# Two steps' attention sums in one run, and a state space's narrow products padded to 128

## The chip, the cores and the metric

The kernel runs on one core of a Trainium2 chip. The metric is the device time of one execution in microseconds. A core has a matrix engine (PE, with its weight loads listed apart as PEld), a vector engine (DVE), a scalar engine for activation functions (ACT), a general engine (POOL), a queue engine (SP), and DMA queues. The engines run side by side and wait for one another through semaphores. Products are written to PSUM, which has eight banks here; everything else lies in SBUF.

## The reference

Two layers over one sequence of 2048 positions with 128 channels, all in 32-bit floating point. Each of four blocks normalises, computes and adds to the residual:

```python
x = x + L0_attn(layernorm(x))   # state space, 8 heads of 32, state 16, gated
x = x + L0_ffn(layernorm(x))    # causal attention, 16 heads of 8, then 8 experts
x = x + L1_attn(layernorm(x))   # second state space, 256 channels, state 16
x = x + L1_ffn(layernorm(x))    # feed-forward, 512 hidden
```

The change touches the first state space and the attention. Their cores are:

```python
# state space, per position t
h = exp(dt*A) * h + dt * x_t[..., None] * B_t          # B_t, C_t: 16 values
y_t = einsum('bhpn,bn->bhp', h, C_t) + D * x_t
# attention
scores = einsum('bqhd,bkhd->bhqk', q, k) / sqrt(8)     # causal mask
out = einsum('bhqk,bkhd->bqhd', softmax(scores), v)
```

## The kernel before

The sequence is cut into four chunks c of 512 positions, each of four blocks of 128. A tile framework turns the program, written in the order of its priorities, into one list of instructions for each engine, with waits; within an engine the list runs in order.

**Stages.** First the state space (`ssd(c)`) for chunks 0 and 1 runs alone, with the preparation of attention for chunk 0. Then the state space for chunks 2 and 3 runs beside the attention of chunks 0 and 1; `abreast` deals out turns to both in proportion to their lengths. Then the attention of chunks 2 and 3 runs alone, with small extra pieces (the preparation of chunk 3, output products, the experts' gates). Experts, second state space and feed-forward follow.

**State space.** Within a chunk, the scan is done block by block with matrix products. For each block b: four products of 128 rows (taps of the convolution, L623) and one product of a single row, which adds the bias `cb_half` (L624), make `xbc`, 288 wide: 256 channels, 16 columns of B, 16 of C. B and C are transposed by products with 16 weight columns (L645) into `bcT`, 16 partitions high. Their product (L649) contracts over 16 rows; 128-row products make the decay matrix (L640) and the output within the block (L665). The product with the old state (L671) contracts over 16 rows; the new state (L678) is a product with 16 weight columns. In a trace the shape of a product is given as rows*columns of the array that it uses: 1*128, 16*128, 128*16 and 128*128. `xbc` and `bcT` come from the pool of work tiles, `state` from the pool of small tiles, each with two buffers.

**Attention.** Heads go in groups g of four (NG = 4 groups). `prepare(c)` writes keys `kR` and queries `qR`, laid out so that each head has 32 rows. Two threads of work follow.

- `shift` computes the scores of queries against keys once (L311, with a mask product L320 where the chunk is on the diagonal) only for their maxima. VectorE reduces each bank (L317, L321), and `spread` turns the maxima into a row `sh`. The bank is tag `m`: two buffers in the mixed stage, three in attention alone.
- `weighted` goes through the key blocks kb of 128. One step computes transposed scores for four heads, in two pairs (L395), adds the maxima (L401) and on the diagonal a mask (L404), and takes the exponential on ACT (L406) into `probs`. The bank is tag `e`, two buffers, one per pair.

`sum_up` multiplies one step's exponentials by the values, with 9 weight columns per head, or 32 for the first block (L363), and accumulates over the key blocks in the bank of tag `o`. One step has four such products, each of which the hardware's list holds as two instructions. After the last key block the sums are copied out (L369), and `end_group` transposes and divides them (L375, L380).

What sets the order: `attentions` takes one turn of the maxima for each of the six turns of a step, so a step's list on PE is two score products, a maximum's product, two additions of the maxima, another maximum's product, the same for the second pair, and then the sums of the step before, which `weighted` keeps in the list `waiting`:

```python
                if i and waiting:
                    sum_up(*waiting.pop())
            waiting.append((c, g, kb, q0, prs, last))
```

So each step of 160 (16 for each group of chunk 3, 12, 8 and 4 for those of chunks 2, 1 and 0) has one run of sums. `probs` has five buffers: two steps of two, and one more. `qR` has 12 buffers, three chunks of four groups.

Of the kernel before, what the change touches and what calls it, by code (L numbers as in the profile page):

```python
# [12 lines left out]
F32 = mybir.dt.float32  # L13
BF16 = mybir.dt.bfloat16
F32R = mybir.dt.float32r
AF = mybir.ActivationFunctionType
# [56 lines left out]
def two_layers(ctx: ExitStack, tc: tile.TileContext, a: dict, out: bass.AP):  # L73
# [186 lines left out]
    def prepare(c, bank):  # L260

        xn = xa[c] = xp.tile([P, NB, D], F32, tag="xa", name="xa", bufs=4)
        layernorm(xn, xc[c])
        nx = aw.tile([P, NB, D], F32, tag="os", name="nx")
        layernorm(nx, xn)
        nc.gpsimd.tensor_tensor(xn, xn, row("bo").unsqueeze(1).to_broadcast([P, NB, D]), ALU.add)
        pt = transposed(nx, bank)
        nT = aw.tile([P, C], F32, tag="nTa", name="nTa", bufs=1)
        nc.vector.tensor_scalar(nT, pt, col("ln1_w"), col("ln1_b"), ALU.mult, ALU.add)
        yield 1.0  # L270
        pv = bank([P, NB, NH, HD])
        for b in range(NB):
            nc.tensor.matmul(
                pv[:, b].rearrange("p h d -> p (h d)"), nT[:, b * P : (b + 1) * P], w_v, start=True, stop=True
            )
        for b in range(NB):
            kb = c * NB + b
            nc.vector.tensor_tensor(
                (v0 if kb == 0 else vv[:, kb - 1])[:, :, 0:HD], pv[:, b], row("bv").rearrange("p (h d) -> p h d", h=NH), ALU.add
            )  # L280
        yield 1.0
        cs = slice(c * C, (c + 1) * C)
        held[c] = []
        for g in range(NG):
            held[c].append(ap.tile([P, C], F32R, tag="qR", name="qR", bufs=3 * NG))
            for w, n, dst in ((w_k, "k", kR[:, g, cs]), (w_q, "q", held[c][g])):
                pf = bank([P, C])
                nc.tensor.matmul(pf, w[:, g], nT, start=True, stop=True)
                hi = aw.tile([P, C], F32R, tag="os", name="hi")
                nc.scalar.activation(hi, pf, AF.Identity, bias=col(f"b{n}", g))  # L290
                yield 1.0
                nc.tensor.matmul(pf, minus[n], hi, start=False, stop=True, skip_group_check=True)
                nc.vector.tensor_scalar(dst, pf, col(f"b{n}", g), None, ALU.add)
# [89 lines left out]
    def weighted(c, g):  # L383

        qR = held[c][g]
        sh = held.pop((c, g))
        for kb in range((c + 1) * NB):
            diag = kb >= c * NB
            q0 = (kb - c * NB) * P if diag else 0
            prs = []  # L390
            for i in range(0, 4, 2):
                pss = psum("e", [P, 2, C])
                for j in range(2):
                    hr = slice(32 * (i + j), 32 * (i + j) + 32)
                    nc.tensor.matmul(  # L395
                        pss[:, j, q0:], kR[hr, g, kb * P : (kb + 1) * P], qR[hr, q0:], start=True, stop=False
                    )
                yield
                for j in range(2):
                    hr = slice(32 * (i + j), 32 * (i + j) + 32)  # L400
                    nc.tensor.matmul(pss[:, j, q0:], onesR[hr], sh[hr, q0:], start=False, stop=not diag)  # L401
                yield
                for j in range(2 * diag):
                    nc.tensor.matmul(pss[:, j, q0 : q0 + P], ident16, mask_kq, start=False, stop=True)  # L404
                pr = ak.tile([P, 2, C], F32, tag="probs", name="probs", bufs=5)
                last = nc.scalar.activation(  # L406
                    pr[:, :, q0:], pss[:, :, q0:], AF.Exp, scale=float(1.0 / np.sqrt(np.float32(HD)))
                )
                in_turn("exp", last)
                prs.append(pr)  # L410
                yield
                if ending:
                    end_group(*ending.pop())
                if i and waiting:
                    sum_up(*waiting.pop())
            waiting.append((c, g, kb, q0, prs, last))

    def conclude(c):
# [25 lines left out]
    def attentions(*which):  # L444


        if not at["maxima"]:
            take(sizes[0] + LEAD)
        for c, g in which:
            if g == 0 and c:  # L450
                extras.append(conclude(c - 1))
            if (c, g) == (NC - 2, 0):
                extras.append(prepare(NC - 1, lambda shape: psum("m", shape)))
            if (c, g) == jobs[-1]:
                extras.extend(gating(i, lambda shape: psum("m", shape)) for i in range(NC - 1))
            for n, _ in enumerate(weighted(c, g)):
                next(ahead, None)
                if n % 3 < 2:
                    continue
                at["softmax"] += 1  # L460
                at["maxima"] += 1
                if n % 6 == 5:
                    while at["maxima"] + 2 <= np.interp(at["softmax"] + LEAD, starts[:-1], starts[1:]):
                        take(2)
                    if n > 6 and extras and next(extras[0], None) is None:
                        extras.pop(0)
                yield 1.0
        for e in extras:
            for _ in e:
                pass  # L470
        extras.clear()
        sum_up(*waiting.pop())
        end_group(*ending.pop())

    ahead = maxima(jobs)
# [58 lines left out]
    with ExitStack() as first:  # L534
# [9 lines left out]
        w_xbc = load(wp, "w_xbc", [P, XBC])  # L544
        nc.vector.tensor_scalar(w_xbc, w_xbc, 0.5, None, ALU.mult)
        nc.vector.tensor_tensor(w_tap, w_tap, w_xbc.unsqueeze(1).to_broadcast([P, 4, XBC]), ALU.mult)
        cb_half = wp.tile([1, XBC], F32, name="cb_half")
        nc.vector.tensor_scalar(cb_half, row("conv_b", 1), 0.5, None, ALU.mult)
        w_dt = load(wp, "w_dt", [P, NH0])
        w_zx = load(wp, "w_zx", [P, 2 * DI])  # L550
        nc.vector.tensor_scalar(w_zx[:, 0:DI], w_zx[:, 0:DI], 0.5, None, ALU.mult)
# [13 lines left out]
        nc.gpsimd.memset(halo0, 0.0)  # L565

        state = [None]

        big, small_bank = (lambda shape: psum("a", shape)), (lambda shape: psum("c", shape))

# [5 lines left out]
        def ssd(c):  # L576
# [43 lines left out]
            for b in range(NB):  # L620
                pc = big([P, XBC])
                for k in range(4):
                    nc.tensor.matmul(pc, nT[:, b * P + k : (b + 1) * P + k], w_tap[:, k, :], start=k == 0, stop=False)  # L623
                nc.tensor.matmul(pc, ones[0:1, :], cb_half, start=False, stop=True)  # L624
                xbc = work([P, XBC], "xbc", "xbc")
                nc.scalar.activation(xbc, pc, AF.Tanh)
                nc.vector.scalar_tensor_tensor(xbc, xbc, 1.0, pc, ALU.add, ALU.mult)
                xh = xbc[:, 0:DI].rearrange("p (h q) -> p h q", h=NH0)

                r = work([P, NH0, P], "r", "ssd_r")  # L630
# [9 lines left out]
                    nc.tensor.matmul(pr, after, r[:, 4 * j : 4 * j + 4, :].rearrange("p h t -> p (h t)"), start=True, stop=True)  # L640
                    nc.scalar.activation(m[:, 4 * j : 4 * j + 4, :].rearrange("p h t -> p (h t)"), pr, AF.Exp)
                yield 3.6
                pb = small_bank([DS, 2, P])
                for j in range(2):
                    nc.tensor.matmul(pb[:, j, :], xbc[:, DI + j * DS : DI + (j + 1) * DS], ident, start=True, stop=True)  # L645
                bcT = work([DS, 2, P], "bcT", "bcT")
                nc.vector.tensor_copy(bcT, pb)
                pcb = small_bank([P, P])
                nc.tensor.matmul(pcb, bcT[:, 0, :], bcT[:, 1, :], start=True, stop=True)  # L649
                cb = work([P, P], "cb", "cb")  # L650
# [18 lines left out]
                if old is not None:  # L669
# [4 lines left out]
                    yi = work(hd, "yi", "yi")  # L674
                    nc.vector.tensor_tensor(yi, pi, dec[:, 0, b, :].unsqueeze(2).to_broadcast(hd), ALU.mult)
                    nc.gpsimd.tensor_tensor(yb, yb, yi, ALU.add)
                pn = small_bank([DS, NH0, HD0])
                nc.tensor.matmul(  # L678
                    pn.rearrange("p h q -> p (h q)"), xbc[:, DI : DI + DS], xw.rearrange("p h q -> p (h q)"), start=True, stop=True
                )  # L680
                new = sp.tile([DS, NH0, HD0], F32, tag="state", name="state")
                if old is None:
                    nc.vector.tensor_copy(new, pn)
                else:
                    nc.vector.tensor_tensor(
                        new, old, dec[:DS, 1, b, :].unsqueeze(2).to_broadcast([DS, NH0, HD0]), ALU.mult
                    )
                    nc.vector.tensor_tensor(new, new, pn, ALU.add)
                state[0] = new
                yield 2.8  # L690

# [34 lines left out]
        with ExitStack() as mixed:  # L726
            psum_of(mixed, "psum1", e=1, m=2, o=1, a=2, c=1)
            ak = attending.enter_context(tc.tile_pool(name="attention_work", bufs=2, side="right"))
            pools.update(
                work=mixed.enter_context(tc.tile_pool(name="work1", bufs=1)), bufs=dict(t512=2, xbc=2, bcT=2, cb=2, xdt=2, xw=2, xd=2, yi=2), other=1  # L730
            )
            for _ in abreast(
                (attentions(*jobs[0 : 2 * NG]), starts[2 * NG], 1.0),
                (then(prepare(1, big), ssd(2), prepare(2, big), ssd(3)), 20.0 + 2 * SSD, 1.0),
            ):
                pass
# [404 lines left out]
```

## Time and profile before

| | us |
|---|---|
| median of 3 runs | 1590.36 |
| range of the 3 runs | 1579.39 to 1594.73 |
| the profiled execution, its own time | 1590.13 |
| span of the profiled execution | 1588.4 |
| mean granted TensorE clock in it | 0.879 |

The span runs from the first to the last instruction. The groups that the change concerns, as the profile lists them for the whole span (times are busy time):

| line, what | count | busy us |
|---|---|---|
| L363 sums of attention (PE) | 1152 + 128 | 169.8 + 37.3 |
| L311 products for the maxima (PE) | 640 | 248.5 |
| L317, L321 reductions to the maxima (DVE) | 384 + 256 | 245.7 + 116.9 |
| L395, L401 scores of a step (PE) | 640 + 640 | 150.0 + 129.7 |
| L406 exponentials (ACT) | 320 | 279.5 |
| L624 bias, one row (PE) | 32 | 14.3 |
| L645 transposes of B and C (PE) | 64 | 9.9 |
| L649 C times B (PE) | 32 | 7.9 |
| L671 old state (PE) | 30 | 13.8 |
| L678 new state (PE) | 32 | 12.8 |

Several products can run in the array at once, so busy times of PE lines overlap. A timeline line gives the start, the time from the first start to the last end of the instructions merged in it, engine, line, operation, out<-in, the array's rows*columns, the operand's size and the count; in brackets stands the idle time of the engine before it and what ended that. A line of a table of windows gives the window, its length, then for PE, PEld, DVE, ACT and POOL busy time and number of instructions, then the granted clock as a share of full speed, the DMA share and GB/s.

### The profile page before, as it was taken

To read this page: it belongs to the slowest core of one execution; us is meant where nothing else is said; L and a number is where in the kernel's file an instruction comes from. 1 tells how busy PE (TensorE), PEld (TensorE's weight loads), DVE (VectorE), ACT (ScalarE), POOL (GpSimd) and SP (SyncE) were. 2 spreads that over 40 slices of the span, in tenths; PEclk is the share of its full clock that TensorE was granted. 3 is DMA by queue.
4 is the path that set the end of the run, shared out by engine and by line. 5 is a ranking of instruction groups with operands and counts; after the bars stand their busy time and mean duration, and the time that the engine had idled before them with its cause. 6 is when DMAs were issued, how large, how long until landed. Compare 5 with 4: busy or idle time off the path is not lost. (4 is left out here: it accounts for less than half of the span.)

```text
span 1588.4 us, 16815 instructions
## 1 busy us (share of the span) xinstructions
PE 1407.8 (89%) x6318; PEld 632.5 (40%) x6318; DVE 978.8 (62%) x1850; ACT 660.3 (42%) x819; POOL 276.0 (17%) x303
## 2 busy tenths in 40 slices
PE   5888999999999999999999997998699797588968
PEld 3554544444344343333333334433233333334423
DVE  4544665446555466677778722247856889868950
ACT  2211152123533234554566663437365554454601
POOL 3322102111111010000000000113322542413210
PEclk9877698578988679788999997999899998898979
DMA  3000000000000000000000003336665765845931
GB/s 94 0 1 1 0 1 1 1 1 1 1 0 1 0 19 0 1 1 1 1 1 1 1 2 107 107 103 156 139 151 142 156 156 115 189 107 148 193 70 33
DMA packets 64978, 87.51 MB, mean 55 GB/s; under 512 B 4992, under 2 KB 29216, under 8 KB 64896
## 3 DMA queue, kind: packets, MB, share of 16 engines
q1 hardware_dynamic: 50320, 58.10, 12.2%
q0 software_dynamic: 14144, 27.27, 10.1%
q10 hardware_dynamic: 432, 1.06, 0.2%
q8 instruction: 50, 0.82, 0.2%
q14 instruction: 32, 0.26, 0.1%
HBM read 57.90 MB, written 1.25 MB: 37 GB/s over the span
## 5 line engine op out<-in xcount | busy, mean ns | idle before, releaser
L406 ACT ACTIVATE probs<-ps_e 128x1024 f32<-128x1024 f32 (+3 forms) x320 | 279.5, 895 | 326.3 <-PE ps_e L404 127.6
L317 DVE TENSOR_REDUCE top<-ps_m 128x1 f32<-128x512 f32 x384 | 245.7, 685 | 80.1 <-PE ps_m L311 74.7
L311 PE MATMUL ps_m<-kR,qR 32*128 32x512 f32 (+3 forms) x640 | 248.5, 498 | 26.1 <-DVE top L317 17.3
L924 DVE TENSOR_TENSOR_SCAN db<-da,hlast,db 128x512 f32<-128x512 f32 x128 | 165.1, 1335 | 26.6 <-ACT da L920 25.8
L363 PE MATMUL ps_o<-probs,vv 128*9 128x512 f32 (+3 forms) x1152 | 169.8, 541 | 0.0
L321 DVE TENSOR_REDUCE top<-ps_m 128x1 f32<-128x128 f32 (+3 forms) x256 | 116.9, 486 | 85.6 <-PE ps_m L320 84.9
L395 PE MATMUL ps_e<-qR,kR 32*128 32x512 f32 (+3 forms) x640 | 150.0, 480 | 2.8 <-ACT probs L406 1.9
L311 PEld LDWEIGHTS ps_m<-kR,qR 32*128 32x128 f32 x640 | 103.1, 201 | 110.1 <-DVE top L317 56.6
L846 PE MATMUL ps_c<-h,wide 128*128 128x512 f32 x256 | 126.3, 633 | 17.7 <-DVE ye L850 13.8
L840 PE MATMUL ps_a<-nT,wide 128*128 128x512 f32 x256 | 126.8, 626 | 4.6 <-ACT h L841 2.6
L401 PE MATMUL ps_e<-sh,onesR 32*128 32x512 f32 (+3 forms) x640 | 129.7, 402 | 0.0
L841 ACT ACTIVATE h<-ps_a,cols 128x512 f32<-128x512 f32 x128 | 86.5, 687 | 97.1 <-PE ps_a L840 96.7
L395 PEld LDWEIGHTS ps_e<-qR,kR 32*128 32x128 f32 x640 | 62.0, 195 | 150.5 <-ACT probs L406 89.8
L846 PEld LDWEIGHTS ps_c<-h,wide 128*128 128x128 f32 x256 | 50.5, 202 | 86.6 <-issue 59.3
L922 DVE TENSOR_TENSOR db<-du,bb 128x1024 f32<-128x1024 f32 x64 | 79.1, 1254 | 0.0
L840 PEld LDWEIGHTS ps_a<-nT,wide 128*128 128x128 f32 x256 | 44.7, 195 | 76.3 <-ACT h L841 46.7
L920 ACT ACTIVATE da<-dl 128x1024 f32<-128x1024 f32 x64 | 64.1, 1049 | 15.9 <-DMA db<-db 11.6
L428 POOL TENSOR_TENSOR x<-x,xa 128x512 f32<-128x512 f32 x4 | 5.1, 1269 | 377.6 <-DVE xa L427 194.6
L401 PEld LDWEIGHTS ps_e<-sh,onesR 32*128 32x128 f32 x640 | 68.9, 203 | 2.1 <-issue 1.3
L852 POOL TENSOR_TENSOR acc<-acc,ye 128x512 f32<-128x512 f32 x28 | 47.3, 1689 | 124.1 <-DVE ye L850 120.0
L998 PE MATMUL ps_f<-g,wide 128*128 128x512 f32 x128 | 59.7, 617 | 7.5 <-ACT g L1004 3.8
L928 POOL COPY hlast<-db 128x2 f32<-128x2 f32 x48 | 34.4, 717 | 183.0 <-DVE db L924 182.0
(296 smaller groups left out, 1989.4 us busy)
## 6 DMA issues: line engine op xcount, KB each, us to landing
wide<-in_fc SPq DMA_DIRECT2D x64, 256.0 KB, 3.2
bb<-scratch_b SPq DMA_DIRECT2D x64, 256.0 KB, 4.2
db<-db POOLq DMA_DIRECT2D x28, 512.0 KB, 6.4
u<-db POOLq DMA_DIRECT2D x24, 512.0 KB, 6.4
gb<-scratch_g SPq DMA_DIRECT2D x32, 256.0 KB, 5.1
wide<-in_h SPq DMA_DIRECT2D x16, 512.0 KB, 5.5
wide<-in_w SPq DMA_DIRECT2D x8, 256.0 KB, 5.2
x<-in_x SPq DMA_DIRECT2D x4, 256.0 KB, 5.3
```

Of the source, the lines that this page charges most:

```text
L311: nc.tensor.matmul(pss[:, 0:n], qR[hr, w - P : w], kR[hr, g, kc * C : kc * C + n], start=True, stop=not diag)
L317: nc.vector.tensor_reduce(top[:, i, kc : kc + 1], pss, AX.X, ALU.max)
L321: nc.vector.tensor_reduce(top[:, i, kc : kc + 1], pss[:, 0:n], AX.X, ALU.max)
L363: pv = nc.tensor.matmul(o, v, prs[i // 2][:, i % 2, q0:], start=kb == 0, stop=kb == nk - 1)
L395: nc.tensor.matmul(pss[:, j, q0:], kR[hr, g, kb * P : (kb + 1) * P], qR[hr, q0:], start=True, stop=False)
L401: nc.tensor.matmul(pss[:, j, q0:], onesR[hr], sh[hr, q0:], start=False, stop=not diag)
L406: last = nc.scalar.activation(pr[:, :, q0:], pss[:, :, q0:], AF.Exp, scale=float(1.0 / np.sqrt(np.float32(HD))))
L840: nc.tensor.matmul(ph, we[:, 0, f * P : (f + 1) * P], nT, start=True, stop=True)
L841: in_turn("gelu", nc.scalar.activation(hs[f // 2][:, f % 2, :], ph, AF.Gelu, bias=col("fc1_b", e * NF + f)))
L846: nc.tensor.matmul(py, we[:, 1, f * P : (f + 1) * P], hs[f // 2][:, f % 2, :], start=f == 0, stop=f == NF - 1)
L922: nc.vector.tensor_tensor(db, du, bb.unsqueeze(1).to_broadcast(two), ALU.mult)
L924: nc.vector.tensor_tensor_scan(db[:, j, :], da[:, j, :], db[:, j, :], hlast[:, j, n : n + 1], ALU.mult, ALU.add)
```

## The change

There are two parts.

**Sums of two steps in a row.** `weighted` no longer sums at every step. At each even key block it sums all the steps that are waiting, which are the two before it, oldest first; at odd key blocks it sums nothing. The number of key blocks is even, so a group's last two are summed at the next group's first step. To hold the results, `probs` gets seven buffers; to make room, `qR` gets eight.

```diff
-            held[c].append(ap.tile([P, C], F32R, tag="qR", name="qR", bufs=3 * NG))
+            held[c].append(ap.tile([P, C], F32R, tag="qR", name="qR", bufs=2 * NG))
...
-                pr = ak.tile([P, 2, C], F32, tag="probs", name="probs", bufs=5)
+                pr = ak.tile([P, 2, C], F32, tag="probs", name="probs", bufs=7)
...
-                if i and waiting:
-                    sum_up(*waiting.pop())
+                while i and kb % 2 == 0 and waiting:
+                    sum_up(*waiting.pop(0))
...
-        sum_up(*waiting.pop())
+        while waiting:
+            sum_up(*waiting.pop(0))
```

**The state space's narrow products.** The bias, `xbc`, `bcT` and the state get tiles of full height or greater width, which POOL fills with zeros once at the start; the tiles are taken in turn, two of each. The products then use 128 rows and 128 columns; copies and activations touch the same part as before.

```diff
-        cb_half = wp.tile([1, XBC], F32, name="cb_half")
-        nc.vector.tensor_scalar(cb_half, row("conv_b", 1), 0.5, None, ALU.mult)
+        cb_half = wp.tile([P, XBC], F32, name="cb_half")
+        nc.gpsimd.memset(cb_half, 0.0)
+        nc.vector.tensor_scalar(cb_half[0:1], row("conv_b", 1), 0.5, None, ALU.mult)
...
+        WIDE = XBC - DS + P
+        wides = {"xbc": (2, [P, WIDE]), "bcT": (2, [P, 2, P]), "state": (2, [P, NH0, HD0])}
+        for tag, (n, shape) in wides.items():
+            wides[tag] = [wp.tile(shape, F32, name=f"{tag}{i}") for i in range(n)]
+            for t in wides[tag]:
+                nc.gpsimd.memset(t, 0.0)
+
+        def wide(tag):
+            wides[tag].append(wides[tag].pop(0))
+            return wides[tag][-1]
...
-                nc.tensor.matmul(pc, ones[0:1, :], cb_half, start=False, stop=True)
-                xbc = work([P, XBC], "xbc", "xbc")
+                nc.tensor.matmul(pc, ones, cb_half, start=False, stop=True)
+                xbc = wide("xbc")
+                xv = xbc[:, 0:XBC]
...
-                pb = small_bank([DS, 2, P])
+                pb = small_bank([P, 2, P])
                 for j in range(2):
-                    nc.tensor.matmul(pb[:, j, :], xbc[:, DI + j * DS : DI + (j + 1) * DS], ident, start=True, stop=True)
-                bcT = work([DS, 2, P], "bcT", "bcT")
-                nc.vector.tensor_copy(bcT, pb)
+                    nc.tensor.matmul(pb[:, j, :], xbc[:, DI + j * DS : DI + j * DS + P], ident, start=True, stop=True)
+                bcT = wide("bcT")
+                nc.vector.tensor_copy(bcT[0:DS], pb[0:DS])
...
-                pn = small_bank([DS, NH0, HD0])
+                pn = small_bank(hd)
                 nc.tensor.matmul(
-                    pn.rearrange("p h q -> p (h q)"), xbc[:, DI : DI + DS], xw.rearrange("p h q -> p (h q)"), start=True, stop=True
+                    pn.rearrange("p h q -> p (h q)"), xbc[:, DI : DI + P], xw.rearrange("p h q -> p (h q)"), start=True, stop=True
                 )
-                new = sp.tile([DS, NH0, HD0], F32, tag="state", name="state")
+                new = wide("state")
```

The product with the old state (L671) is unchanged in its text; its operands `bcT` and `old` are now 128 partitions high. The updates of the new state act on its first 16 partitions.

More of the change, by code (lines that the diff above doesn't have):

```diff
@@ L623, in ssd @@
                     nc.tensor.matmul(pc, nT[:, b * P + k : (b + 1) * P + k], w_tap[:, k, :], start=k == 0, stop=False)
-                nc.tensor.matmul(pc, ones[0:1, :], cb_half, start=False, stop=True)
-                xbc = work([P, XBC], "xbc", "xbc")
-                nc.scalar.activation(xbc, pc, AF.Tanh)
-                nc.vector.scalar_tensor_tensor(xbc, xbc, 1.0, pc, ALU.add, ALU.mult)
+                nc.tensor.matmul(pc, ones, cb_half, start=False, stop=True)
+                xbc = wide("xbc")
+                xv = xbc[:, 0:XBC]
+                nc.scalar.activation(xv, pc, AF.Tanh)
+                nc.vector.scalar_tensor_tensor(xv, xv, 1.0, pc, ALU.add, ALU.mult)
                 xh = xbc[:, 0:DI].rearrange("p (h q) -> p h q", h=NH0)
@@ L676, in ssd @@
                     nc.gpsimd.tensor_tensor(yb, yb, yi, ALU.add)
-                pn = small_bank([DS, NH0, HD0])
+                pn = small_bank(hd)
                 nc.tensor.matmul(
-                    pn.rearrange("p h q -> p (h q)"), xbc[:, DI : DI + DS], xw.rearrange("p h q -> p (h q)"), start=True, stop=True
+                    pn.rearrange("p h q -> p (h q)"), xbc[:, DI : DI + P], xw.rearrange("p h q -> p (h q)"), start=True, stop=True
                 )
-                new = sp.tile([DS, NH0, HD0], F32, tag="state", name="state")
+                new = wide("state")
                 if old is None:
-                    nc.vector.tensor_copy(new, pn)
+                    nc.vector.tensor_copy(new[0:DS], pn[0:DS])
                 else:
                     nc.vector.tensor_tensor(
-                        new, old, dec[:DS, 1, b, :].unsqueeze(2).to_broadcast([DS, NH0, HD0]), ALU.mult
+                        new[0:DS], old[0:DS], dec[:DS, 1, b, :].unsqueeze(2).to_broadcast([DS, NH0, HD0]), ALU.mult
                     )
-                    nc.vector.tensor_tensor(new, new, pn, ALU.add)
+                    nc.vector.tensor_tensor(new[0:DS], new[0:DS], pn[0:DS], ALU.add)
                 state[0] = new
@@ L729, in two_layers @@
             pools.update(
-                work=mixed.enter_context(tc.tile_pool(name="work1", bufs=1)), bufs=dict(t512=2, xbc=2, bcT=2, cb=2, xdt=2, xw=2, xd=2, yi=2), other=1
+                work=mixed.enter_context(tc.tile_pool(name="work1", bufs=1)), bufs=dict(t512=2, cb=2, xdt=2, xw=2, xd=2, yi=2), other=1
             )
```

## The prediction

> **What bounds the kernel now.** I read the page first, then a table of stages, then the instructions in order of time in the stage that the change is about, then the granted clock there.
>
> ```profile
> span 1588.4 us, 16815 instructions
> PE 1407.8 (89%) x6318; PEld 632.5 (40%) x6318; DVE 978.8 (62%) x1850; ACT 660.3 (42%) x819; POOL 276.0 (17%) x303
> ```
> ```profile
> 27.00:185.00 158.00, 138.03 (x522) 82.50 (x521) 82.07 (x201) 26.84 (x46) 39.10 (x48) 0.80 0.00 1
> 185.00:575.00 390.00, 381.24 (x1872) 178.41 (x1874) 215.02 (x516) 122.91 (x174) 49.47 (x61) 0.82 0.01 3
> 575.00:965.00 390.00, 364.23 (x2642) 147.23 (x2637) 266.63 (x562) 215.93 (x252) 8.90 (x11) 0.91 0.00 1
> 965.00:1588.40 623.40, 515.76 (x1267) 218.93 (x1267) 404.30 (x523) 288.43 (x338) 168.40 (x155) 0.92 0.55 132
> ```
>
> The table gives, after the length of each stage, busy time of PE, PEld, DVE, ACT and POOL, then the granted clock. The stages are state space alone, state space beside attention's first two chunks, attention alone, everything later. The last is not touched. PE looks like the bound in the other three, so the next view is one step of attention alone, in order of time.
>
> ```profile
> 835.58 1.05 PE L363 MATMUL ps_o<-probs,vv 128*9 128x512 f32 x8
> 836.56 0.50 PE L395 MATMUL ps_e<-qR,kR 32*128 32x512 f32 x2
> 836.57 0.51 PE L311 MATMUL ps_m<-kR,qR 32*128 32x512 f32 x2
> 836.89 0.39 PE L401 MATMUL ps_e<-sh,onesR 32*128 32x512 f32 x2
> 836.90 0.40 PE L395 MATMUL ps_e<-qR,kR 32*128 32x512 f32 x2
> 837.12 0.39 PE L311 MATMUL ps_m<-kR,qR 32*128 32x512 f32 x1
> 837.13 0.40 PE L401 MATMUL ps_e<-sh,onesR 32*128 32x512 f32 x2
> 837.88 0.49 PE L311 MATMUL ps_m<-kR,qR 32*128 32x512 f32 x1 [0.34 <-DVE top L317]
> 838.30 1.04 PE L363 MATMUL ps_o<-probs,vv 128*9 128x512 f32 x8
> ```
> ```profile
> 834.42 2.48 DVE L317 TENSOR_REDUCE top<-ps_m 128x1 f32<-128x512 f32 x4 [0.23 <-PE ps_m L311]
> 837.13 2.48 DVE L317 TENSOR_REDUCE top<-ps_m 128x1 f32<-128x512 f32 x4 [0.23 <-PE ps_m L311]
> ```
>
> A plain step (no mask) takes 2.72 us from sums to sums (835.58 to 838.30). It isn't PE's alone. The fourth maximum's product waits 0.34 us for a bank that VectorE frees; VectorE works 2.48 of the 2.71 us (four reductions, 0.62 each) and then waits 0.23 us for PE. The loop runs bank free, fourth product, sums, next step's first product, reduction.
>
> **What a change of array shape costs.** In the state space's products:
>
> ```profile
> 27.86 2.10 PE L623 MATMUL ps_a<-w_tap,nT 128*128 128x288 f32 x8
> 29.89 0.75 PE L624 MATMUL ps_a<-cb_half,ones 1*128 1x288 f32 x2
> 30.57 1.12 PE L640 MATMUL ps_a<-ssd_r,after 128*128 128x512 f32 x2
> ```
>
> One L623 lasts about 0.406 us at full clock (its line's median), so seven pitches share 2.10-0.41 and the pitch is 0.24: a product starts 0.165 before the end of the one before it. At the two changes (L623 to L624, L624 to L640) it starts only 0.07 before. A change costs 0.095 us. The Trainium skill (TensorEngine Tiling (Array Packing), Tiling Modes) says that changing the tiling mode drains the engine, and its page TensorE: Matmul & The Clock Gate (Part 2) puts a drain at about 128 cycles, 0.053 us at its 2.4 GHz. By the page every saving below would be little more than half; I use the row.
>
> **The change part by part.**
>
> *State space alone (27 to 185 us, 8 blocks).* Counting neighbours in the trace's order, 104 changes of shape lie here and 36 would be left with the padded shapes; 61 of the 68 removed have no idle PE before them. 61 x 0.095 = 5.8 us. The two L624 also take 0.68 from start to start of the next, against 2 x 0.24 at full rows, 0.2 in all with 0.1 of it beyond the entry; L649 and L671 are alike. That is about 0.3 a block, 2.4 us. Total 8 us. PE isn't always the chain: it idles for some 20 of 158 us behind VectorE, and some of the gain goes there. I take -6 (0 to -9). Wider weights in L645 and L678 (16 to 128 columns) raise a load from 0.096 to 0.19 us, hidden beside the products: L711, the same 128x128 product with full weights, has a mean of 287 ns against L645's 275. The copies and activations stay at their old sizes.
>
> *Memsets.* Seven more on POOL: by the rows of its memsets (128x512 0.51 us, 128x128 0.20) about 2.3 us, beside an idle stretch of 3.9 us before the first normalisation's POOL step at 8.38 us. Nothing; at most 2.3 if they were queued behind that step. The write of cb_half waits for one of them, at 7.38 us and so behind that cover too.
>
> *State space beside attention (185 to 575 us).* Here the small shapes stand next to attention's 32-row products and share their shape. Padded, 12 changes more lie in this stretch (506 to 518): +1.2 us. The inner gain of 0.3 a block gives -2.4. Of 48 runs of sums 24 are merged. Most stand beside 128-row mask products, so a merge saves one change, some two: 24 x 0.13 = -3. Together -4 (-8 to +3).
>
> *Tile counts.* qR falls from three chunks' worth to two. Chunk 2's first write comes with L288 at 391 us; chunk 0's attention is closed by L426 at 344.6. Chunk 3's is at 604.7, chunk 1's closing products are near 589. The cover is 46 and 15 us: nothing. probs rises from 5 to 7, which the two held steps need: nothing.
>
> *Sums of two steps in a row, attention alone.* A run of 16 products lasts 0.87 us longer (two pitches of 1.05-0.60, rounded down), and every second step has none. In the loop above, the next step's first product then comes 0.87 later: VectorE, with only three banks to read, waits 0.23+0.87 = 1.10 us once a pair instead of 0.23 twice. A plain pair takes 8 x 0.62+1.10 = 6.06 against 5.43: +0.6. ScalarE is queued behind the same run, its next scores being later, but its two exponentials take 1.94 of 2.72 us, so VectorE is late first. About 20 pairs of the 96 steps with maxima are plain: +12. The 28 others have masks, are PE's, and save a way in and a way out, 0.2 each, less some starvation: -4. The last group (8 pairs, no maxima) saves 1.6 and gives it back to ScalarE. Together +8 (-12 to +25; the low end is the case that the reductions never starve).
>
> *The clock.* Three stretches of 3.41 us at the end of a group:
>
> ```profile
> 821.64:825.06 3.42, 3.17 (x31) 1.40 (x30) 3.38 (x6) 1.59 (x4) 0.00 (x0) 1.00 0.00 0
> 825.06:828.47 3.41, 3.16 (x31) 2.01 (x31) 2.48 (x7) 2.72 (x4) 0.00 (x0) 1.00 0.02 5
> 828.47:831.88 3.41, 3.41 (x23) 1.18 (x21) 0.98 (x5) 1.02 (x1) 0.00 (x0) 0.50 0.00 0
> ```
>
> The clock fell to half after 825.06:828.47, where no PE idle exceeds 0.25 us. What was low there is streaming: with 0.22 us for a 512-wide group of scores (836.90 to 837.12) and 0.42 for a group of sums, its products stream about 1.6 us, 0.47 of it; in a plain step 4 x 0.22+2 x 0.42 = 1.72 of 2.72, 0.63. The window that ended the half clock streamed over 0.8. The skill's clock page (Part 1; Why this matters for your kernels) says cold follows an idle window of about 3.4 us and warns of PE gaps over about 3 us. By that rule the merge costs no clock, since no such gap exists. By the trace it does: between two runs of a plain pair lie 4.2 us that stream 8 x 0.22 = 1.76, 0.42 of the time, and a window inside falls under one half. Of the positions of a window in 6.0 us, (0.8+2 x 0.42)/6.0 = 0.27 do. So about one drop in two pairs, some 20 in 48 pairs, each of one or two windows, 6 us: 120 us cold. Today the stage from 589.5 to 912 has clock 0.93, so 45 us. A cold pair streams 3.4 us more, 9.3 against 6.06, so each cold microsecond loses 0.35: 75 x 0.35 = +26 (-10, if the long run instead ends cold spells sooner, to +60).
>
> **Sum:** -6-4+8+26 = +24 on the profiled execution's 1590.13 us (span 1588.4, the rest around it), which is also the median of 1590.36: 1614 us.
>
> **Rivals.** *Faster:* PE is the bound everywhere and drains are what counts. Then 80 merges and the padding give -6-4-56 x 0.2 = -21, and with less cold time 20 x 0.35 = -7: about 1562. For it: PE at 93% and 98% in two stages. Against: the waits for VectorE in every plain step. It decides if the reductions keep work through the double run: three banks are 3 x 0.62 = 1.86 us, and bank to reduction would take about 2.9. If the first of the two sums were placed one product earlier, it could. *No change:* the clock doesn't care, -6-4+8 = -2, 1588; the same if the order of instructions, which a scheduler sets (in the mixed stage runs of sums are split two and six), pulls the two sums apart. *Cold for good:* half of 322 us at half clock, (161-45) x 0.35 = +41, with 10 more in the mixed stage and +8-10: about 1640, up to 1680.
>
> **Numbers.** Chances: the forecast 0.50 (its own range 1595 to 1640), faster 0.14, no change 0.22, cold for good 0.14. The range 1572 to 1668 leaves about one in ten on either side. One per cent, about what a measurement of this kernel can tell from no change, is 16 us: faster 0.14, within 0.26, slower 0.60.
>
> **What would show it.** Right: L363 in runs of 16 and VectorE's wait on L311 near 1.1 us once a pair; more half-clock slices between 590 and 912 us, clock near 0.82; the stage 27 to 185 some 6 us shorter. Wrong: the stage 575 to 965 no longer than 390 us, or its clock still at 0.91.

## The result: slower, and the profile after

The changed kernel takes 1648.88 us (median of 4 runs, 1635.56 to 1652.14) against 1587.21 us (median of 4, the three runs above and one more); the ratio is 1.037, interval 1.029 to 1.045. Here and below, ratios, their intervals and the profiles that are read leave out executions more than 1.5 per cent above the fastest of the same kernel, and medians are of all. The direction was the forecast one, the size was not: +62 us where +24 was forecast. The page of the changed kernel begins:

```profile
span 1650.4 us, 16809 instructions
PE 1469.8 (89%) x6318; PEld 679.1 (41%) x6318; DVE 976.2 (59%) x1850; ACT 661.6 (40%) x819; POOL 277.2 (17%) x310
```

PE has the same 6318 products and is busy 62 us longer, at the same share of the span. The same products took longer. The next lines are tables of windows, first of the kernel before, then of the changed one. The stages are now cut at the first score product of `weighted`, at the closing product of chunk 1 and at the last sum, so that each line holds the same work in both.

```profile
27.00:169.30 142.30, 123.56 (x481) 74.97 (x479) 71.08 (x164) 26.84 (x46) 37.83 (x46) 0.83 0.00 1
169.30:590.00 420.70, 409.53 (x1976) 192.60 (x1974) 236.45 (x591) 127.76 (x179) 53.56 (x68) 0.79 0.01 2
...
590.00:961.30 371.30, 349.32 (x2572) 139.72 (x2570) 253.84 (x511) 210.26 (x244) 6.07 (x7) 0.93 0.00 1
```
```profile
27.00:167.10 140.10, 119.43 (x484) 83.72 (x482) 72.95 (x165) 27.32 (x47) 38.36 (x47) 0.82 0.00 1
167.10:581.00 413.90, 401.90 (x1972) 202.38 (x1970) 234.56 (x588) 127.40 (x179) 53.24 (x67) 0.80 0.01 2
...
581.00:1026.30 445.30, 428.39 (x2576) 170.37 (x2574) 252.03 (x515) 212.01 (x244) 6.36 (x7) 0.78 0.00 1
```

State space alone is 2 us shorter, state space beside attention 7 us shorter, and attention alone 74 us longer; what follows is 3 us shorter (627.1 to 624.1). Sum +62. In the long stage the work of VectorE and ScalarE is the same; what differs is the granted clock, 0.93 before and 0.78 after. The trace's clock records have only two values, full and half. Summed over the stage, the half clock lasts 54.6 us in 7 stretches before and 193.7 us in 26 after, the first of them begun before the stage.

A plain pair of steps of the changed kernel, and VectorE's reductions in it, in order of time:

```profile
829.87 1.90 PE L363 MATMUL ps_o<-probs,vv 128*9 128x512 f32 x16
...
833.02 0.50 PE L311 MATMUL ps_m<-kR,qR 32*128 32x512 f32 x1 [0.34 <-DVE top L317]
833.62 0.50 PE L395 MATMUL ps_e<-qR,kR 32*128 32x512 f32 x2
833.62 0.50 PE L311 MATMUL ps_m<-kR,qR 32*128 32x512 f32 x1
833.96 0.40 PE L401 MATMUL ps_e<-sh,onesR 32*128 32x512 f32 x2
834.22 0.50 PE L311 MATMUL ps_m<-kR,qR 32*128 32x512 f32 x1
...
835.84 3.30 PE L363 MATMUL ps_o<-probs,vv 128*9 128x512 f32 x16
```
```profile
832.28 4.87 DVE L317 TENSOR_REDUCE top<-ps_m 128x1 f32<-128x512 f32 x8 [1.02 <-PE ps_m L311]
```

The run of 16 is there, and so is the wait of VectorE, 1.02 us once in a pair. The pair lasts 5.97 us at full clock, against 5.43 for two plain steps before. The next run of 16 takes 3.30 us instead of 1.90, because the clock has fallen meanwhile. The windows of the clock there:

```profile
829.37:832.79 3.42, 3.31 (x30) 1.03 (x28) 2.40 (x6) 1.63 (x3) 0.00 (x0) 1.00 0.02 5
832.79:836.20 3.41, 2.99 (x17) 1.33 (x21) 3.41 (x7) 3.41 (x4) 0.00 (x0) 1.00 0.00 0
836.20:839.61 3.41, 3.41 (x20) 0.86 (x14) 0.95 (x2) 0.28 (x1) 0.00 (x0) 0.50 0.00 0
```

The middle window lies between the two runs of sums: 17 products in 3.41 us, the last four of them the first of the next run, and no idle time of PE above 0.4 us. Half clock follows. The third window holds a run of sums at half clock, and after it the clock is full again.

**How windows stream.** From each product's start, its columns and the granted clock one can work out for how much of a window anything streams through the array (an estimate, with the 0.22 us of a group of scores and the 0.42 us of a group of sums from the trace before; some records are missing). Among windows at full clock in this stage the mean is the same before and after, about 0.64; the spread is not, standard deviation 0.085 and 0.12. The windows just ahead of a fall to half clock have a median of 0.47 before and 0.52 after, those just ahead of a return 0.88 and 0.91. By this estimate full clock is lost near one half and given back only above some 0.8. It is no sharp limit: after the change, falls followed windows of some 0.43 to 0.63, and a few windows below 0.6 kept the full clock.

### The profile page after: what moved, and what is told of

Read it like the earlier page. It is cut to its first block, busy times and chain, and to the rows that moved or that the text cites. A ratio compares the mean times of both kernels' runs of the same rounds, so it can differ in the third digit from the quotient of the medians.

```text
span 1650.4 us, 16809 instructions
## 1 busy us (share of the span) xinstructions
PE 1469.8 (89%) x6318; PEld 679.1 (41%) x6318; DVE 976.2 (59%) x1850; ACT 661.6 (40%) x819; POOL 277.2 (17%) x310
## 5 line engine op out<-in xcount | busy, mean ns | idle before, releaser
L311 PE MATMUL ps_m<-kR,qR 32*128 32x512 f32 (+3 forms) x640 | 275.4, 530 | 19.1 <-DVE top L317 10.1
L363 PE MATMUL ps_o<-probs,vv 128*9 128x512 f32 (+3 forms) x1152 | 198.5, 656 | 0.0
L395 PE MATMUL ps_e<-qR,kR 32*128 32x512 f32 (+3 forms) x640 | 168.4, 504 | 5.6 <-ACT probs L406 3.5
L311 PEld LDWEIGHTS ps_m<-kR,qR 32*128 32x128 f32 x640 | 114.2, 212 | 127.4 <-DVE top L317 50.4
L401 PE MATMUL ps_e<-sh,onesR 32*128 32x512 f32 (+3 forms) x640 | 140.8, 420 | 0.0
L395 PEld LDWEIGHTS ps_e<-qR,kR 32*128 32x128 f32 x640 | 68.5, 204 | 129.7 <-issue 76.9
L401 PEld LDWEIGHTS ps_e<-sh,onesR 32*128 32x128 f32 x640 | 73.3, 212 | 4.0 <-issue 2.9
L363 PEld LDWEIGHTS ps_o<-probs,vv 128*9 128x9 f32 x1152 | 31.0, 101 | 87.1 <-issue 81.9
```

The source lines that it names most:

```text
L311: nc.tensor.matmul(pss[:, 0:n], qR[hr, w - P : w], kR[hr, g, kc * C : kc * C + n], start=True, stop=not diag)
L363: pv = nc.tensor.matmul(o, v, prs[i // 2][:, i % 2, q0:], start=kb == 0, stop=kb == nk - 1)
L395: nc.tensor.matmul(pss[:, j, q0:], kR[hr, g, kb * P : (kb + 1) * P], qR[hr, q0:], start=True, stop=False)
```

## The experiments

The experiments below were timed beside the kernel before on the same chips (its medians there 1583 to 1586 us). "Half clock" is its time in attention alone. "Full-clock part" is the stage less 0.42 us for each us at half clock. The 0.42 comes from two profiles of the same attention: the changed kernel's stage of 445.3 us with 193.7 us at half clock, and that of the sums alone, 420.4 us with 134.7 us: (445.3-420.4)/(193.7-134.7). That these two have the same full-clock part, 364, is so by construction; that the kernels with one step's sums at every step and no product twice all come out at 348 to 350 is not.

The granted clock is on record for every execution, and since it has two values, it gives the time at half clock (an estimate: twice the missing share of the span). Over 167 executions, each compared with the others of its kernel, the time rises by 0.39 us with each us at half clock, with a correlation of 0.99: this is nearly all of the spread between runs. The medians are 371 us at half clock before (339 to 399 in 33 runs on one chip), 504 in the changed kernel, 502 in the sums alone, and 339 and 341 with the padding alone. The changed kernel's 133 us more, at 0.42, are 56 of its 62.

| kernel | median us | ratio to before (interval) | stage us | half clock us | full-clock part us |
|---|---|---|---|---|---|
| before | | | 371.3 | 54.6 | 348 |
| changed | 1648.9 | 1.037 (1.029 to 1.045) | 445.3 | 193.7 | 364 |
| sums alone | 1647.3 | 1.037 (1.031 to 1.043) | 420.4 | 134.7 | 364 |
| padding alone | 1571.9 | 0.984 (0.980 to 0.988) | | | |
| padding alone, again | 1572.1 | 0.992 (0.988 to 0.995) | 371.8 | 54.6 | 349 |
| tile counts alone | 1585.5 | 1.001 (0.998 to 1.003) | 375.3 | 64.9 | 348 |
| sums held, one run a step | 1598.9 | 1.009 (1.007 to 1.012) | 367.1 | 45.0 | 348 |
| both sums in the even step, apart | 1617.2 | 1.021 (1.017 to 1.026) | 398.7 | 116.5 | 350 |
| sums alone, scores twice | 1662.0 | 1.047 (1.042 to 1.053) | 431.2 | 126.8 | 378 |
| sums alone, odd scores thrice | 1674.9 | 1.059 (1.055 to 1.064) | 442.0 | 113.6 | 394 |
| before, scores twice | 1602.7 | one run | 388.8 | 30.7 | 376 |
| pairs in chunks 0, 1 only | 1604.1 | 1.014 (1.008 to 1.019) | 366.8 | 44.5 | 348 |
| the same, with padding | 1576.7 | 0.993 (0.990 to 0.995) | 371.0 | 49.0 | 350 |

**The parts one by one.** The sums alone leave out the state space's hunks of the diff, the padding alone leaves out the four hunks of attention, and the counts alone keep only `2 * NG` and `bufs=7`.

```diff
# sums alone, against the kernel before
-                if i and waiting:
-                    sum_up(*waiting.pop())
+                while i and kb % 2 == 0 and waiting:
+                    sum_up(*waiting.pop(0))
... (the other three hunks of attention as in the changed kernel)
```

> The sums of two steps in a row with the changed tile counts, the state space as before. If the loss is attention's alone, this is slower than before by 65 to 75 us (the whole 62 and what the padding gained), with the stage of attention alone near 440 us and about 190 us of it at half clock. Rival: if the padding has a part in the loss, this is slower by less than 50 us.

> Only the state space's products padded to 128; attention as before. By the prediction's terms (6 us where the state space is alone, 4 beside attention) 1577 to 1583 us against 1587. Rival: the changes of array shape that the padding adds beside attention eat it, and it is within 3 us of before.

> Only the tile counts changed: eight buffers of queries, seven of exponentials; sums at every step. Prediction: no change, within 0.5 per cent. Rival: fewer query buffers make a write wait for the last reader, some us slower; or more buffers of exponentials let ScalarE run ahead and it is faster.

The sums alone cost 62 us; the padding alone gains 13 (medians 1571.9 and 1585.1), more than the 4 to 10 that were expected, and the counts do nothing. So the loss is attention's. The sum of the parts, +62-13 = +49, isn't the +62 of the whole. The granted clocks say where the 13 went: the padding alone has some 31 us less at half clock, which at 0.42 is all of its gain but 1 or 2 us, and between the sums alone and the changed kernel there is no such saving (502 and 504 us). In their two profiles the padding does save 49 us of half clock beside the state space (217 to 168), but attention alone has 59 more (135 to 194), with the same code; why isn't known. The expected length of the stage was met by the changed kernel and missed by the sums alone, 420 us instead of 440; its stage beside the state space is longer instead, 431.4 us.

**Is it the merging or the holding?** One kernel holds the exponentials just as long, but sums one step at each step; a group's closing pieces come a step later for it.

```diff
# against the sums alone
-                while i and kb % 2 == 0 and waiting:
+                if i and len(waiting) > 1:
                     sum_up(*waiting.pop(0))
...
-                    if n > 6 and extras and next(extras[0], None) is None:
+                    if n > 12 and extras and next(extras[0], None) is None:
```

> Sums held for two steps as in the sums-only kernel, with its buffers, but one step's sums at every step: as many changes of array shape as before and no long run (a group's closing pieces are dealt out one step later). Theory (the merging, not the holding, is what costs): back to the kernel before, 1575 to 1600 us, stage of attention alone 365 to 380 us with 50 to 80 us at half clock. Rival (the older exponentials, the later end of a group and the fuller buffers cost): stays above 1620 us.

It is back at 1.009; the stage of attention alone is even 4 us shorter than before. Holding isn't the cause of the large loss. The 0.9 per cent that stay lie ahead of that stage, which starts at 600 instead of 590 us.

**Long run or uneven stream?** The next kernel keeps both sums in the even step, but one after each pair of heads. No run is longer than before, and nothing is saved on changes of shape.

```diff
# against the sums alone
-                while i and kb % 2 == 0 and waiting:
+                if kb % 2 == 0 and waiting:
                     sum_up(*waiting.pop(0))
```

> Both held steps' sums still in the even step, but apart: one after its first pair, one after its second; the odd step has none. Runs of 8 again, as many changes of shape as before, and VectorE is not starved for 1.02 us at once. Starvation theory: back near the kernel before, under 1605 us. Clock theory: between the second run and the next first one some 4 us still stream under one half, so the stage keeps over 110 us at half clock and the kernel stays above 1615 us.

Its runs in a stretch at full clock, and then the stage as a whole:

```profile
862.39 1.05 PE L363 MATMUL ps_o<-probs,vv 128*9 128x512 f32 x8
864.02 1.05 PE L363 MATMUL ps_o<-probs,vv 128*9 128x512 f32 x8
867.88 1.05 PE L363 MATMUL ps_o<-probs,vv 128*9 128x512 f32 x8
```
```profile
596.60:995.30 398.70, 385.86 (x2575) 150.51 (x2574) 253.50 (x511) 212.81 (x243) 5.24 (x7) 0.85 0.00 1
```

From the first run of one pair to the first run of the next is 5.49 us, no longer than before (2.72 and 2.93, 5.65, for a plain step and one with masks). At full clock it costs nothing; its full-clock part is 350 us against 348. Yet the stage is 27 us longer with 116.5 us at half clock. So the loss needs neither a long run nor a starved VectorE: an uneven stream, some 3 us without sums and then two runs close together, is enough to slow the clock. The starvation theory, which asked for under 1605 us, falls for this kernel.

**Filling the stretch.** Two kernels compute score products again, over their own result, to stream more where sums are missing. The third does the same to the kernel before, as a control.

```diff
# sums alone, scores twice (chunks 2 and 3)
-                    nc.tensor.matmul(
-                        pss[:, j, q0:], kR[hr, g, kb * P : (kb + 1) * P], qR[hr, q0:], start=True, stop=False
-                    )
+                    for n in range(2 if c > 1 else 1):
+                        nc.tensor.matmul(
+                            pss[:, j, q0:], kR[hr, g, kb * P : (kb + 1) * P], qR[hr, q0:], start=True, stop=n == 0 and c > 1
+                        )
# odd scores thrice: range(3 if c > 1 and kb % 2 else 1), the stop to match
```

> The sums of two steps in a row as in the first kernel, and in chunks 2 and 3 each product of a step's scores (L395) is computed twice, the second over the first: 448 products of up to 512 columns more for PE, no result changed. Clock theory: the stretch between two runs of sums now streams about 2.6 of 4.5 us instead of 1.76 of 4.2, so fewer windows fall under one half; half-clock time in the stage falls from 190 us to under 100 and the kernel is 15 to 40 us FASTER than the first kernel although PE has more to do. Rival (VectorE's starvation and PE's length are what costs, the clock is by the way): PE's list grows by 0.44 us a step, so it is 0 to 45 us SLOWER than the first kernel.

> The sums-only kernel, and in chunks 2 and 3 the score products of the odd steps alone (the ones without sums) computed three times, where PE waits for VectorE. The full-clock plain pair should stay near 6.0 us, the stretch between runs streams 2.6 of 4.3 us. Clock theory: half-clock time in the stage of attention alone falls below 100 us (sums-only: 135, changed kernel: 194) and the stage below 410 us (420 and 445). Rival (what a window streams is not what the clock follows): half-clock time as in the sums-only kernel, stage not shorter.

> The kernel before, with the score products of every step of chunks 2 and 3 computed twice. A control for the doubled products without the merging: PE has 0.34 us of waiting in a plain step, the doubling adds 0.44. Stage of attention alone 371 us before; if the doubling costs its full length in steps that PE sets and 0.1 in the others, 385 to 400 us at the same half-clock time of some 55 us; if it also keeps the clock up, less.

The gains that the clock theory promised did not come: both fillings are slower than the sums alone, by 15 and 28 us. The columns of the table say why: the filling isn't hidden, it lengthens the full-clock part by 14, 30 and 28 us. The half clock was to fall under 100 us and has 126.8 and 113.6. That is less than the 134.7 and 193.7 of the two kernels without filling, but these two have the same attention code and lie 59 us apart, so the fall is not shown. In the control it goes from 54.6 to 30.7, the lowest of all kernels in the table, in one run. So what exactly the clock follows, the share that streams or the short waits themselves, stays argued. A cheaper filling was not tried.

**Beside the state space.** Here the merging was to gain 3 us.

```diff
# pairs in chunks 0, 1 only: against the sums alone; with padding: against the changed kernel
-                while i and kb % 2 == 0 and waiting:
+                while i and (c > 1 or kb % 2 == 0) and waiting:
```

> Two steps' sums in one run only in chunks 0 and 1, beside the state space; chunks 2 and 3 sum at every step; no padding. The prediction's term is -3 us for the 24 merges. Rival, from the sums-only kernel, whose stage beside the state space was 431 us with 217 us at half clock (before: 421 and 174): the merges cost the clock here too, +8 to +15 us.

> The padding, and the merged sums only in chunks 0 and 1: the changed kernel without what hurts in the stage of attention alone. If the attention of chunks 2 and 3 carries the whole loss, this keeps the padding's gain, 1568 to 1578 us, and the stage of attention alone is back at 365 to 380 us. Rival: the merges beside the state space cost as well, 1580 to 1600 us.

> The padding alone once more, beside the one with merged sums in chunks 0 and 1, to compare them on one chip: 1570 to 1578 us; faster than before by 8 to 20 us as the first time. If the first gain was the chance of half-clock stretches, within 5 us of before.

Pairs in chunks 0 and 1 alone cost 18 us. The stage beside the state space grows from 420.7 to 432.8 us, with its half clock from 174 to 215 us, the same as in the sums alone (431.4 and 217). With the padding, the same pairs cost about 5 us (1576.7 against 1572.1), which the intervals don't separate. The padding alone is the fastest version seen, faster than both kernels. With 0.42 taken here too (the kernel before and the tile counts, which have the same work in this stage, give 0.43), the two stages part into clock and the rest:

| kernel | state space alone us | half clock us | full-clock part us | beside attention us | half clock us | full-clock part us |
|---|---|---|---|---|---|---|
| before | 142.3 | 47.8 | 122 | 420.7 | 174 | 348 |
| sums alone | 142.7 | 51.2 | 121 | 431.4 | 217 | 340 |
| pairs in chunks 0, 1 only | 147.4 | 61.4 | 122 | 432.8 | 215 | 343 |
| padding alone, again | 136.3 | 44.4 | 118 | 398.7 | 113 | 351 |
| pairs in chunks 0, 1, padding | 138.2 | 47.8 | 118 | 415.4 | 170 | 344 |
| changed | 140.1 | 51.2 | 119 | 413.9 | 168 | 343 |

At full clock the merging does save 5 to 8 us beside the state space; the clock takes more. The padding saves about 4 us where the state space is alone and loses about 3 beside attention, for a cause that no run here shows; in that stage its gain is less time at half clock. The padding's products at the place shown before:

```profile
30.39 2.10 PE L636 MATMUL ps_a<-w_tap,nT 128*128 128x288 f32 x8
32.33 0.65 PE L637 MATMUL ps_a<-cb_half,ones 128*128 128x288 f32 x2
32.81 1.88 PE L654 MATMUL ps_a<-ssd_r,after 128*128 128x512 f32 x4
```

From the first tap product to the decay product is 2.42 us, 2.71 before: 0.29 gained on the bias alone.

## Why the prediction was right in kind and wrong in size

- **State space alone, -6.** Measured 142.3 to 136.3 us with the padding alone: near enough, some 4 of it at full clock and the rest less time at half clock. In the changed kernel the stage shows 140.1; there the half clock was 51.2 us instead of 44.4.
- **Beside the state space, -4.** In the changed kernel's profile -7, some 4 of it at full clock. The total was luck: at full clock the merging gives more than its -3 and the padding takes some back. And the clock, which has no term here, costs the merging 17 us in the kernel with pairs in chunks 0 and 1 only (41 us more at half clock), for +12 in all.
- **Tile counts, memsets: nothing.** Right: 1.001 for the counts; the seven memsets end at 5.5 us on POOL and its first normalisation step starts at 8.73 us, set by the load and VectorE.
- **Starvation of VectorE, +8.** The loop was right: the wait of 1.10 us was measured as 1.02, the plain pair of 6.06 as 5.97. The sum was wrong, +16 (364 less 348), because the pairs with masks were to give 4 back. A group of chunk 3 shows it, from one L333 to that of the next group, in the kernel before and in the sums alone:

```profile
820.54:868.23 47.69, 44.31 (x367) 17.38 (x365) 38.29 (x73) 29.97 (x34) 0.00 (x0) 0.96 0.01 1
```
```profile
856.95:914.94 57.99, 56.12 (x367) 22.44 (x365) 37.47 (x72) 30.31 (x34) 0.00 (x0) 0.82 0.00 1
```

The group has 3.4 us at half clock before and 20.5 in the sums alone, so at 0.42 it is 3 us longer at full clock. Its two plain pairs give 1.1 of this; the other 2 come from pairs with masks. One kind of these takes what it took before (5.66 us, 941.23 to 946.89 in the changed kernel, against 2.72+2.93), but the pair before a group's last takes 7.45 us (849.24 to 856.69 in the sums alone) against 6.11 (861.86 to 867.97 before); 0.2 of that difference are sums that stood in a neighbouring pair. And the changed kernel's trace has 9 pairs without a mask product where about 20 were counted: plain steps mostly stand beside steps with masks.
- **The clock, 75 x 0.35 = +26: this is the term that failed.** The mechanism was right, the size was not. The profile has 139 us more at half clock, not 75, and each costs 0.42, not 0.35: +58, which with the 16 makes the stage's 74. In the sums alone the same attention code had 80 us more, +34, and +16: near its +49. The number of falls was about right (25 and 22 where some 20 were counted). But the 75 is the 120 us of those falls less the 45 of today, as if the falls of today would go. Most of them stay, and some grow: the one at the end of a group of chunk 3 lasts 3.4 us before (from 828.47) and 10.2 in the sums alone (862.1 to 872.3). And most of the half clock, some 120 of the 194 us, falls in pairs with masks, which the estimate took for plain ones. That the long run ends cold spells sooner, the low end of the range, has little for it: stretches last 7.4 and 6.0 us on average against 7.8 before, but there are three times as many.
- **Which rule decided.** By the rule of the Trainium skill (TensorE: Matmul & The Clock Gate, Part 1), that cold follows an idle window, the merge would have been free; the windows ahead of the 25 falls have no idle time of PE above 0.8 us, and the measurement decides. The page's other statement, that one sees two states of the clock, half and full, holds in every record here.
- **The rival "cold for good"** put the half clock at half of the stage and the time at 1640. It was nearest in size; its share, 194 of 445 us, is 0.43.

What stays open is what exactly the clock follows, how the padding comes to save half clock, and why the changed kernel spends that saving again in attention alone.

## What to carry to other kernels

Before products are gathered into longer runs to save changes of array shape (0.1 us each), look at what is left between the runs: if PE there waits in small pieces for another engine, the same mean load can lose the full clock. In this kernel even spreading was worth more than the saved changes. Where narrow products stand among full ones, padding them to the full shape gained 4 us of 142 at full clock; beside attention's 32-row products it gained nothing at full clock. Most of the padding's 13 us was less time at half clock, and together with the sums in pairs everywhere that gain was not there. So before two gains are added, see whether both are the clock's.

## What the runs showed of the hardware

- Full clock can be lost without a long idle gap. In attention alone it fell after windows of 3.41 us in which products streamed about half of the time (an estimate) and PE was never idle for over 0.8 us, and it came back after windows that streamed over about 0.8. A microsecond at half clock cost 0.42 us in attention alone, and 0.39 over all executions.
- The same instructions can have 135 or 194 us at half clock in a stage of some 400 us, and 339 to 399 us in the whole of one kernel. The second spread is 25 us of time, so a single execution of such a kernel is uncertain by that much.
- Two 288-column products with a single row, between products of 128 rows, took 0.68 us from their start to that of the next product, both changes of shape in it; padded to 128 rows with zeros they took 0.48.
